# Layer 3 attention written out in order on three engines, with the router's logits on VectorE

## The chip, the cores and the metric

The kernel runs on one NeuronCore of one Trainium2 chip. The metric is device time in microseconds, the time of one launch; the median of several runs is given with the lowest and the highest. A profile is one further execution under the hardware profiler. Its span begins and ends with the program's instructions, so its own run time is a little longer than the span. The engines are called by the profile's names: PE is TensorE (PEld its weight loads), ACT ScalarE, DVE VectorE, POOL GpSimd, SP SyncE.

## The reference, cut to what matters

The network has four layers. The change concerns the last one, whose two parts work on 8 samples of 1024 tokens with 256 channels:

```python
def layer3_attention(x):                 # x: 8 x 1024 x 256
    q, k, v = heads(layernorm(x) @ qkv_w.T + qkv_b)        # 8 heads of 32 channels
    a = (q @ k.T * 32**-0.5 + 5.0) ** 2                    # a square in place of exp
    a = a / a.sum(-1, keepdims=True)
    return x + merge(a @ v) @ proj_w.T + proj_b

def layer3_experts(x):
    tokens = layernorm(x)
    probs = softmax(tokens @ router_w.T)                   # 8 experts
    rw, re = top_k(probs, 2)
    rw = rw / max(rw.sum(-1), 1e-12)
    out = tokens
    for e in range(8):
        h = gelu(tokens @ w1[e] + b1[e])
        out = out + combine[:, e] * (h @ w2[e] + b2[e])
    return x + out
```

This is a condensed form of the reference: bookkeeping (images to tokens, zero biases) is left out. Since a weight is a square of a sum, the sum of a row of `a` is a quadratic form in q, and needs no pass over the weights: with G = the sum over all keys of k times k transposed, head by head, the denominator of a query comes from q, Gq and the sum of the keys. The kernel uses this.

## The kernel before

Each layer is a Python generator that writes instructions; the `yield`s are places at which another generator may be let in. The framework then lays the instructions out, engine by engine, by a schedule of its own, except where a line pins them in program order (`net.pinned`). The order on an engine's queue is fixed when the program is built; at run time each engine works through its queue in order and waits on semaphores.

Layer 3's attention is `fast3` (from L2520), its router and the sorting of tokens by expert is the class `Routes`, and the experts are `fast3e`. Before attention starts, `fast3` loads its weights, normalises sample 0 beside the end of the layer before it (`norm`, L2567), waits for the point `HOLD` at which the other layer gives its space back (L2717), and then makes the products of sample 0 without attention beside it.

*Attention* (`attention`, L2655) does a sample in 32 steps: two halves of 512 queries, two groups of four heads (`c`), eight tiles of 128 keys (`kt`). A step has

- four score matmuls `s<-q,k` (L2686), one for each head, on rows 32h of the array, into two tiles of two PSUM banks each,
- two activations `e<-s` (L2692) on ScalarE, which square 128x1024 scores each,
- four value matmuls `A<-e,v` of the step before it (L2670), on columns 32h of the array, which add up in one bank over the eight key tiles. After the eighth, VectorE multiplies by the reciprocal denominator, `o<-A,r` (L2675). At the end of a half, PE projects four token tiles into a pair of banks, `proj<-o`, and VectorE adds them to x (`x<-proj,x`, L2681).

The scores and every other product take their tiles from one pool, `own["S"]`, of three tiles of two banks; `own["A"]` has two tiles of one bank. That is all eight banks.

*Beside attention* of sample b, `between(b)` (L2702) writes the router of sample b-1, the normalisation of sample b+1 and its products. `spread` (L1067) deals these pieces out over the 33 yields of `attention(b)`.

- `norm`: the load of x, statistics and normalisation on VectorE (`tn_s`, `tn_m`, `xt<-x,tn_r`), a logarithm and an exponential on ScalarE between them (`tn_r`), 16 transposes on PE (`xn<-ident,xt`) with two copies on VectorE, and the addition of the projection's bias to x on GpSimd (L2582, 128x2048).
- `projections`: q and k (each two pieces with an activation of 1024 columns), v (two pieces with a VectorE copy), the transposes of k (`kT`, two pieces with a VectorE copy), G, then Gq and the sums over a head D, two pieces each, with a VectorE product and two ScalarE functions behind them.
- `Routes.route` (L2380): a second normalisation (`mo_x`), stores of it and of x plus it (the addition on GpSimd, L2391), 16 transposes `mo_xT`, logits as 16 pairs of matmuls `mo_l`, the softmax and the choice of two experts by comparisons on VectorE, and two small matmuls `mo_n` that count the tokens ahead.
- `Routes.fill` (L2359), in sample 0 alone: six DMAs that fill the three tables of sorted rows with zeros, issued from SyncE.
- `Routes.sort` (L2462): in samples 3 and 6 the sorting of a group of three samples: loads of token tiles `xl<-mox` on SyncE and two indirect DMAs for each on GpSimd.

In the last sample the loads of the experts' weights (`net.head()`) stand in place of norm and products. After the loop, the router of the last sample goes beside the first experts: `by_time([[0, 1, some(all_pairs, lead)], [1, 1.1, routing]])` (L2951), where a stream is [first due time, time between pieces, generator].

An expert pair of blocks takes four or eight transposes (`a`), a VectorE copy `xk`, 8 matmuls `h`, a Gelu on ScalarE, matmuls `y`, two VectorE additions, and two indirect DMAs on GpSimd.

Of the kernel before, what the change touches and what calls it, by code (L numbers as in the profile page):

```python
# [17 lines left out]
P = 128  # L18
# [879 lines left out]
class Fast:  # L898
# [123 lines left out]

    def scatter(self, group, after=(), **args):


        made = self.nc.gpsimd.indirect_dma_start(**args)  # L1026
        self.pinned(made)
        ins = made.ins
        self.tc.declare_no_dep(ins, group=group, reason="rows of their own")
        self.tc.add_to_no_dep_group(group, ins)  # L1030
        self.wait_for(ins, after)
        self.groups.setdefault(group, []).append(ins)
# [9 lines left out]
    def pinned(self, *ins):  # L1042
        for i in ins:
            self.tc.keep_in_program_order(i)

# [1263 lines left out]
class Routes:  # L2309
# [28 lines left out]
    def load(self, wp):  # L2338

        net, nc = self.net, self.net.nc  # L2340
        self.wr = net.load(wp, "l3f_wr", "(k p) o -> p k o", p=P)
# [17 lines left out]
    def fill(self):  # L2359
# [8 lines left out]
        for g, so in enumerate(self.sorteds):  # L2368
            self.fills[g] = []
            for lo in range(0, TILES[g], 26):  # L2370
# [5 lines left out]
                self.net.pinned(ins)  # L2376
# [3 lines left out]
    def route(self, b, x, ones, pair):  # L2380
# [8 lines left out]
        yield from net.token_norm_steps(xn, x, two)  # L2389
# [3 lines left out]
        yield  # L2393
        xk = ones.tile([P, KC, N], F32, tag="xn", name="mo_xk")
        for c in range(KC):
            ps = pair("mo_xT").rearrange("p h n -> p (h n)")
            for t in range(NT):
                nc.tensor.transpose(ps[:, bass.ts(t, P)], xn[:, t, bass.ts(c, P)], net.ident)
            nc.vector.tensor_copy(xk[:, c, :], ps)
            yield  # L2400

        pr = two.tile([P, NT, E8], F32, tag="pr", name="pr")
        for t4 in range(0, NT, 4):
            ps = pair("mo_l")[:, 0]
            for i in range(4):
                net.linear(ps[:, bass.ts(i, E8)], xk, self.wr, bass.ts(t4 + i, P), slice(0, E8))
            nc.vector.tensor_copy(pr[:, t4 : t4 + 4], ps[:, : 4 * E8].rearrange("p (t e) -> p t e", e=E8))
            if not t4:
                yield
        red = two.tile([P, NT], F32, tag="red", name="red")  # L2410
        nc.vector.tensor_reduce(red, pr, AX.X, ALU.max)
        nc.vector.tensor_tensor(pr, pr, each(red), ALU.subtract)
        yield
# [11 lines left out]
        nc.vector.tensor_tensor(eq, other, mine, ALU.is_equal)  # L2425
        nc.vector.tensor_tensor(eq, eq, self.before.unsqueeze(1).to_broadcast([P, NT, E8, E8]), ALU.mult)
# [6 lines left out]
        for i in range(2):  # L2433
# [3 lines left out]
            nc.vector.tensor_reduce(weigh[:, i], tmp, AX.X, ALU.add)  # L2437
        nc.vector.tensor_tensor(red, weigh[:, 0], weigh[:, 1], ALU.add)
# [5 lines left out]
        yield  # L2444

        ps = pair("mo_n")[:, 0]
# [10 lines left out]
        for t in range(NT):  # L2457
            nc.vector.tensor_tensor(place[:, t], cnt[:, 0, t], carry, ALU.add)
            nc.vector.tensor_tensor(carry, carry, cnt[:, 1, t], ALU.add)
        yield  # L2460
# [59 lines left out]
def fast3(net, io):  # L2520
# [4 lines left out]
    with ExitStack() as ctx, ExitStack() as tok, ExitStack() as att, ExitStack() as bef:  # L2525
# [3 lines left out]
        def pair(name):  # L2529
            return net.lent["pair"](name) if not own else own["S"].tile([P, 2, HF], F32, tag="S", name=name)  # L2530

        def bank(name):
            return pair(name)[:, 0]
# [28 lines left out]
        xpool = io.pool(tok, "f3x", 3)  # L2562
        one = io.pool(tok, "f3a", 1)
        norms = io.pool(tok, "f3m", 2)
        xs, xns, qs, ks, vs, rs = ({} for _ in range(6))

        def norm(b):  # L2567
            x = xs[b] = xpool.tile([P, NT, C], F32, tag="x", name="x")

            (nc.sync if b else nc.scalar).dma_start(out=halves(x), in_=tokens(io.src[b]))  # L2570
            yield
            xt = one.tile([P, NT, C], F32, tag="xt", name="xt")
            yield from net.token_norm_steps(xt, x, norms, b > 0)
            yield
            xn = xns[b] = one.tile([P, KC, N], F32, tag="xn", name="xn")
            for c in range(KC):
                ps = pair("xn")
                for t in range(NT):
                    nc.tensor.transpose(ps[:, t // 4, bass.ts(t % 4, P)], xt[:, t, bass.ts(c, P)], net.ident)
                nc.vector.tensor_copy(xn[:, c, :], ps.rearrange("p h n -> p (h n)"))  # L2580
                yield
            nc.gpsimd.tensor_tensor(x, x, bo.unsqueeze(1).to_broadcast([P, NT, C]), ALU.add)  # L2582

        def projections(b):
            xn = xns.pop(b)
            for d, w, bias, name in ((qs, wq, bq, "q"), (ks, wkk, bk, "k")):
                d[b] = own["two"].tile([P, KC, N], F32, tag=name, name=name)
                for c in range(KC):
                    ps = pair("qk")
                    for h in range(2):  # L2590
                        net.linear(ps[:, h], w, xn, bass.ts(c, P), bass.ts(h, HF))
                    nc.scalar.activation(d[b][:, c, :], ps.rearrange("p h n -> p (h n)"), AF.Identity, bias=bias(c))
                    yield
            v = vs[b] = own["two"].tile([P, NT, C], F32, tag="v", name="v")
            for t4 in range(0, NT, 4):
                ps = pair("v")
                for i in range(4):
                    net.linear(ps[:, i // 2, bass.ts(i % 2, C)], xn, wv, bass.ts(t4 + i, P), slice(0, C))
                nc.vector.tensor_copy(
                    v[:, t4 : t4 + 4].rearrange("p t c -> p (t c)"), ps.rearrange("p h n -> p (h n)")  # L2600
                )
                yield


            kt = own["k1"].tile([P, NT, KC, P + 4], F32, tag="kt", name="kt")
            nc.gpsimd.memset(kt[:, :, :, P], 1.0)
            for t4 in range(0, NT, 4):
                ps = pair("kT")
                for i in range(4):
                    for c in range(KC):  # L2610
                        nc.tensor.transpose(
                            ps[:, i // 2, (i % 2) * C + c * P : (i % 2) * C + (c + 1) * P],
                            ks[b][:, c, bass.ts(t4 + i, P)], net.ident,
                        )
                nc.vector.tensor_copy(
                    kt[:, t4 : t4 + 4, :, :P], ps.rearrange("p h (i c n) -> p (h i) c n", c=KC, n=P)
                )
                yield
            G = bank("G").rearrange("p (c n) -> p c n", c=KC)
            for c in range(KC):  # L2620
                for t in range(NT):
                    nc.tensor.matmul(
                        G[:, c, : P + 1], lhsT=kt[:, t, c, :P], rhs=kt[:, t, c, : P + 1],
                        start=(t == 0), stop=(t == NT - 1),
                    )
            gm = own["k2"].tile([P, KC, P + 4], F32, tag="gm", name="gm")
            nc.vector.tensor_tensor(gm[:, :, : P + 1], G[:, :, : P + 1], heads.to_broadcast([P, KC, P + 1]), ALU.mult)
            yield
            prod = one.tile([P, KC, N], F32, tag="xt", name="prod")
            r = rs[b] = own["two"].tile([P, KC, N], F32, tag="r", name="r")  # L2630
            for c in range(KC):
                ps = pair("Gq")
                for h in range(2):
                    nc.tensor.matmul(
                        ps[:, h], lhsT=gm[:, c, :P], rhs=qs[b][:, c, bass.ts(h, HF)], start=True, stop=True
                    )
                nc.vector.scalar_tensor_tensor(
                    prod[:, c, :], ps.rearrange("p h n -> p (h n)"), gm[:, c, P : P + 1], qs[b][:, c, :],
                    ALU.add, ALU.mult,
                )  # L2640
                yield
            for c in range(KC):
                ps = pair("D")
                for h in range(2):
# [593 lines left out]
```

## Time and profile before

| | us |
|---|---|
| median of 3 runs | 4155.66 |
| lowest, highest | 4153.86, 4181.26 |
| the profiled execution, its span | 4178.96, 4177.1 |

Shares of the span, from the page:

| engine | busy us | share | instructions |
|---|---|---|---|
| PE | 3826.0 | 92% | 19430 |
| PEld | 1887.8 | 45% | 19430 |
| DVE | 2298.4 | 55% | 3994 |
| ACT | 2260.1 | 54% | 3030 |
| POOL | 566.3 | 14% | 646 |

The mean granted clock of TensorE was 0.954. Three stretches matter here (us from the start of the span; busy time in each):

| stretch | length | PE | DVE | ACT | POOL | clock |
|---|---|---|---|---|---|---|
| end of layer 2, start of layer 3 | 2700 to 2820 | 105.70 | 59.94 | 26.66 | 43.14 | 0.94 |
| attention of layer 3 | 2820 to 3800 | 961.70 | 290.00 | 608.42 | 173.62 | 0.99 |
| experts | 3800 to 4177 | 331.14 | 192.49 | 191.43 | 205.50 | 0.93 |

A busy time is the time in which at least one instruction of the engine was at work. Matmuls overlap, and a matmul that waits inside counts as busy, so 961.70 of 980 says that PE had something in hand nearly always, not that it went at full speed. In lists in order of time, a line gives the start, the length, the engine, the line of the kernel, the operation, what it writes and reads, shape and count, and in brackets how long the engine was idle before it and for whom it waited. One fp32 matmul leaves two records.

The groups that matter in the attention stretch (mean ns of one):

| group | count | mean ns |
|---|---|---|
| `e<-s`, ACT, 128x1024 | 512 | 1111 |
| `o<-A,r`, DVE, 128x512 | 32 | 689 |
| `x<-proj,x`, DVE, 128x1024 | 16 | 1225 |
| `kt<-kT`, `v<-v`, `xn<-xn`, `mo_xk<-mo_xT` copies, DVE, 128x1024 | 14 each | 1225 |
| `x<-x,mo_x` and `x<-x,bo`, POOL, 128x2048 | 8 each | 4537, 4522 |
| layer 2's router `junk<-xn,w_f_wr`, DVE, 128x256 with its accumulator read | 64 | 425 and 83 |
| ACT activation of a bank, 128x512 (`hp<-pi`) and copy (`u<-po`) | 128, 32 | 690, 585 |

### The profile page before, as it was taken

Reading aid. Unit: us, or ns where it says so; the run is one execution under the profiler, and the core shown is the slowest. Engines: PE = TensorE matmul, PEld = TensorE weight load, DVE = VectorE, ACT = ScalarE, POOL = GpSimd, SP = SyncE. Lnnn points to the kernel's source line nnn. Section 1 sums busy time; section 2 is a strip of 40 time slices with the busy share of each in tenths; the row PEclk is TensorE's granted clock in tenths of the full one; section 3 lists DMA queues with packets and bytes.
Section 4 is the critical chain, followed back from the end, with each engine's and each line's share of the span. In section 5 each row is a group of like instructions: output and inputs, shape, how many; then the busy total and the mean of one; then the engine's idle time right before and its main releaser. Section 6 shows DMA issues by size and latency. Waiting matters only on the chain. (4 is left out here: it accounts for less than half of the span.)

```text
span 4177.1 us, 51736 instructions
## 1 busy us (share of the span) xinstructions
PE 3826.0 (92%) x19430; PEld 1887.8 (45%) x19430; DVE 2298.4 (55%) x3994; ACT 2260.1 (54%) x3030; POOL 566.3 (14%) x646
## 2 busy tenths in 40 slices
PE   8999999999878787789999969989899999999987
PEld 3323333333334444454444526653344444346986
DVE  2398798798896489942222356841232333324445
ACT  4556555555553367734334346516566556666554
POOL 0000000000000000000000013430000050124753
PEclk9999999999998889889999979999999999999998
DMA  3313223223131568720000013430700040136676
GB/s 100 113 43 124 90 73 120 88 74 109 62 107 47 185 246 291 264 73 21 21 21 29 22 56 109 142 121 11 219 31 31 9 145 31 37 111 195 202 233 219
DMA packets 210069, 441.13 MB, mean 106 GB/s; under 512 B 22281, under 2 KB 132828, under 8 KB 197396
## 3 DMA queue, kind: packets, MB, share of 16 engines
q1 hardware_dynamic: 186708, 386.17, 28.1%
q0 software_dynamic: 19440, 46.45, 3.3%
q10 hardware_dynamic: 3664, 5.11, 0.4%
q8 instruction: 157, 2.57, 0.3%
q14 instruction: 100, 0.82, 0.1%
HBM read 282.30 MB, written 162.28 MB: 106 GB/s over the span
## 5 line engine op out<-in xcount | busy, mean ns | idle before, releaser
L2692 ACT ACTIVATE e<-s,five 128x1024 f32<-128x1024 f32 x512 | 539.3, 1111 | 280.0 <-PE s L2686 279.2
L1249 DVE SCALAR_TENSOR_TENSOR a<-hp,w_f_vec,a 128x961 f32<-128x961 f32 (+1 forms) x496 | 608.7, 1233 | 115.3 <-ACT a L1242 106.7
L2686 PE MATMUL s<-q,k 32*128 32x512 f32 x2048 | 349.1, 644 | 16.3 <-ACT e L2692 12.1
L1401 ACT ACTIVATE e<-s 128x1024 f32<-128x1024 f32 x256 | 250.2, 1023 | 79.4 <-PE s L1395 62.8
L2670 PE MATMUL A<-e,v 128*32 128x512 f32 x2048 | 279.0, 609 | 0.0
L1355 DVE TENSOR_TENSOR sum<-sum,e 128x1024 f32<-128x1024 f32 x192 | 230.6, 1220 | 87.2 <-ACT e L1401 87.2
L78 PE MATMUL pi<-xn,w_l_wpi 128*128 128x512 f32 x512 | 249.0, 629 | 19.2 <-ACT v L1283 10.0
L1359 PE MATMUL A<-e,va 128*32 128x512 f32 x2048 | 263.0, 610 | 0.0
L2686 PEld LDWEIGHTS s<-q,k 32*128 32x128 f32 x2048 | 111.4, 184 | 179.4 <-issue 96.2
L1395 PE MATMUL s<-q,k 32*128 32x512 f32 x1024 | 181.2, 650 | 2.5 <-ACT e L1401 2.5
L78 PEld LDWEIGHTS pi<-xn,w_l_wpi 128*128 128x128 f32 x512 | 96.7, 199 | 161.9 <-issue 118.2
L2839 PE MATMUL h<-xk,w 128*128 128x128 f32 x1192 | 150.7, 281 | 19.0 <-DVE xk L2825 19.0
L1706 PE MATMUL acc<-wt,z 128*64 128x192 f32 (+4 forms) x1344 | 128.9, 334 | 42.4 <-DVE wt L1761 42.0
L1026 POOL DMA_INDIRECT res<-y,to x149 | 148.4, 996 | 106.6 <-DVE y L2863 47.7
L2839 PEld LDWEIGHTS h<-xk,w 128*128 128x128 f32 x1192 | 148.3, 197 | 24.1 <-DVE xk L2825 19.3
L2808 ACT COPY w<-w_l3f_w 128x512 f32 x149 | 92.6, 625 | 119.6 <-PE h L2839 116.3
L1440 ACT ACTIVATE hp<-pi,pib 128x512 f32<-128x512 f32 x128 | 87.2, 690 | 127.3 <-PE pi L78 127.2
L1310 POOL MEMSET thrice<- 32x128 f32 x32 | 6.3, 196 | 1021.7 <-PE pe L1326 1021.6
L2859 PE MATMUL y<-w_l3f_w,hid 128*128 x596 | 142.8, 382 | 0.3 <-ACT hid L2845 0.3
L1026 POOL DMA_INDIRECT so<-xl,rows x128 | 129.9, 1015 | 93.0 <-issue 51.0
L1706 PEld LDWEIGHTS acc<-wt,z 128*64 128x64 f32 x1344 | 97.7, 151 | 89.5 <-DVE wt L1761 60.1
L1359 PEld LDWEIGHTS A<-e,va 128*32 128x32 f32 x2048 | 57.6, 111 | 174.2 <-issue 172.9
(407 smaller groups left out, 6966.5 us busy)
## 6 DMA issues: line engine op xcount, KB each, us to landing
row<-shifts SPq DMA_DIRECT2D x144, 512.0 KB
x<-d SPq DMA_DIRECT2D x31, 1024.0 KB
xs<-so SPq DMA_DIRECT2D x73, 260.0 KB
so<-zero SPq DMA_DIRECT2D x5, 3380.0 KB
thrice<-vimg SPq DMA_DIRECT2D x64, 256.0 KB
gated<-st SPq DMA_DIRECT2D x32, 512.0 KB
hc<-gated SPq DMA_DIRECT2D x32, 512.0 KB
xl<-mox SPq DMA_DIRECT2D x64, 256.0 KB
```

What stands on the lines that cost most here:

```text
L78: self.nc.tensor.matmul(ps, lhsT=w[:, i, m], rhs=src[:, i, cols], start=(i == 0), stop=(i == k - 1))
L1026: made = self.nc.gpsimd.indirect_dma_start(**args)
L1249: nc.vector.scalar_tensor_tensor(to, fr, taps(t_), to, ALU.mult, ALU.add)
L1355: nc.vector.tensor_tensor(half, half, e[j], ALU.add)
L1359: nc.tensor.matmul(state["A"][32 * h : 32 * h + 32, c, :], lhsT=vas[b][:, kt, c, 32 * h : 32 * h + 32], rhs=e[h // 2][:, h % 2, :], start= ...
L1395: nc.tensor.matmul(ss[h // 2][:, h % 2], lhsT=ks[b][32 * h : 32 * h + 32, bass.ts(kt, P)], rhs=qs[b][32 * h : 32 * h + 32, bass.ts(gq, HF) ...
L1401: nc.scalar.activation(es[i][j], ss[j], AF.Exp, scale=SCALE)
L1706: nc.tensor.matmul(acc[o, a * IMG : e * IMG], lhsT=zs[b][:, c, t, :], rhs=wt[:, c, (a - lo) * IMG : (e - lo) * IMG], start=False, stop=(t ...
L2670: nc.tensor.matmul(A[32 * h : 32 * h + 32], lhsT=v[:, kt, c * P + 32 * h : c * P + 32 * h + 32], rhs=e[:, h, :], start=first, stop=last,)
L2686: nc.tensor.matmul(ss[h // 2][:, h % 2], lhsT=k[32 * h : 32 * h + 32, c, bass.ts(kt, P)], rhs=q[32 * h : 32 * h + 32, c, bass.ts(hh, HF)], ...
L2692: nc.scalar.activation(e[:, 2 * j : 2 * j + 2], ss[j], AF.Square, scale=SCALE, bias=five)
L2839: nc.tensor.matmul(ps[:, j, m], lhsT=ws[j][:, k, bass.ts(m, P)], rhs=xk[:, j, k], start=(k == 0), stop=(k == KC - 1),)
```

## The change

- The attention loop is one loop over 256 steps of all samples (`attention(beside, parts)`), under `net.in_order(PE, DVE, Activation)`: each instruction of these three engines is made to follow the one written before it on its engine.
- Products come in pieces of one bank. `denominators` is split from `projections`; k comes before q. The pieces take their bank from a new pool `own["X"]` of one bank; `own["A"]` shrinks from two tiles to one. A step writes one piece after the values (or a quarter of a sample's projection, one and two steps after the step that follows a half's end), and a further one before the values where the number of the piece is in `SMALL`.
- The copies of the transposes of x (`turned`) and of k go from VectorE to ScalarE.
- The heads of a step are written in the order 2, 3, 0, 1, for scores and values.
- The load of x (`fetch`) is a piece of its own, two samples ahead, at step 10; the normalisation, in small pieces (`token_norm_pieces`), from step 15. Samples 0 and 1 are normalised before the loop.
- The router's logits are 64 multiply-and-sum instructions on VectorE, from a table `f3_wr` of the router's weights repeated on all partitions (1 MB), in place of transposes and matmuls.
- The six fills are written at steps 10, 19, 28, ... and each waits for the last square written before it.
- After the loop, the pieces of the last router come due every 0.26 instead of 1.1.

The core of the diff:

```diff
+    @contextmanager
+    def in_order(self, *engines):
+        traced = self.nc.cur_bb.bb.instructions
+        start = len(traced)
+        yield
+        info = mybir.DependencyInfo(mybir.DependencyClass.NoSync, mybir.DependencyReason.DATA)
+        for engine in engines:
+            last = None
+            for i in traced[start:]:
+                if i.engine == engine:
+                    if last is not None:
+                        self.tc.add_manual_dep(i, last.name, info, reason="as planned")
+                    last = i
...
-                self.net.pinned(ins)
+                self.net.wait_for(ins.ins, [a.ins for a in anchor])
...
-        xk = ones.tile([P, KC, N], F32, tag="xn", name="mo_xk")
-        for c in range(KC):
-            ps = pair("mo_xT").rearrange("p h n -> p (h n)")
-            for t in range(NT):
-                nc.tensor.transpose(ps[:, bass.ts(t, P)], xn[:, t, bass.ts(c, P)], net.ident)
-            nc.vector.tensor_copy(xk[:, c, :], ps)
-            yield
...
+        junk = one.tile([P, C], F32, tag="junk", name="junk")
+        for t in range(NT):
+            for e in range(E8):
+                nc.vector.scalar_tensor_tensor(
+                    junk, xn[:, t, :], 1.0, self.wr[:, e, :], ALU.mult, ALU.mult, accum_out=pr[:, t, e : e + 1]
+                )
+                if e % 2:
+                    yield
...
+        def turned(b, h, c):
...
+            ps = bank("xn")
+            for t in range(4):
+                nc.tensor.transpose(ps[:, bass.ts(t, P)], xts[b][:, 4 * h + t, bass.ts(c, P)], net.ident)
+            nc.scalar.copy(xns[b][:, c, bass.ts(h, HF)], ps)
...
-            for i, (hh, c, kt) in enumerate(steps):
-                ss = [pair("s") for _ in range(2)]
-                for h in range(NH):
+            for i, (b, hh, c, kt) in enumerate(steps):
+                ss = [own["S"].tile([P, 2, HF], F32, tag="S", name="s") for _ in range(2)]
+                for h in LATEST:
...
+                run(i, beside)
+                turn = bool(projects) and projects[0][0] <= i
+                if not turn and parts and parts[0][0] <= i and parts[0][1] in SMALL:
+                    piece()
                 if i:
                     values(i - 1)
-                yield
+                if projects and projects[0][0] <= i:
+                    project(*projects.pop(0)[1:])
+                elif parts and parts[0][0] <= i:
+                    piece()
...
+        LATEST = (2, 3, 0, 1)
+        SMALL = (12, 14, 26)
...
-        own["S"], own["A"] = io.pool(att, "f3s", 3, PSUM), io.pool(att, "f3v", 2, PSUM)
+        own["S"], own["A"] = io.pool(att, "f3s", 3, PSUM), io.pool(att, "f3v", 1, PSUM)
...
+        for i, _ in enumerate(denominators(0)):
+            if 3 <= i < 7:
+                turned(1, (i - 3) // 2, (i - 3) % 2)
+        own["X"] = io.pool(att, "f3o", 1, PSUM)
...
+            if b + 1 < B:
+                parts.append([at + (3 if b else 0), 0, products(b + 1)])
+            if b + 2 < B:
+                beside.append([at + 9, 1, later(1, (fetch(n) for n in (b + 2,)))])
+                beside.append([at + 15, 1, norm(b + 2)])
+            if b:
+                beside.append([at + 3, 0.48, routed(b - 1)])
+            if b == 0:
+                beside.append([at + 10, 9, routes.fill(anchor)])
...
+        with net.in_order(mybir.EngineType.PE, mybir.EngineType.DVE, mybir.EngineType.Activation):
+            attention(beside, parts)
...
-        by_time([[0, 1, some(all_pairs, lead)], [1, 1.1, routing]])
+        by_time([[0, 1, some(all_pairs, lead)], [1, 0.26, routing]])
```

`run(i, beside)` lets in every stream of `beside` that is due at step i; `piece()` writes the next one-bank piece of the products; `products(b)` are `projections(b)`, `denominators(b)` and the four transposes of sample b+1, 30 pieces in all.

## The prediction

> **What bounds the kernel now.** I read first the page's slices, to find the stretch that the change touches, then the table of stretches, then the instructions in order of time. Attention of layer 3 runs from its first score matmul (2819.65 us) to the last addition of the projection (3798.79): 979.1 us of the profiled span of 4177.1. In that stretch the table reads:
>
> ```profile
> 2960.00:3000.00 40.00, 28.82 (x194) 9.47 (x197) 15.20 (x64) 23.17 (x25) 0.00 (x0) 0.86 0.85 270
> 3160.00:3200.00 40.00, 40.00 (x242) 18.50 (x240) 8.59 (x8) 21.78 (x21) 0.32 (x2) 1.00 0.00 1
> 3720.00:3760.00 40.00, 40.00 (x272) 17.32 (x272) 6.54 (x14) 26.50 (x26) 29.39 (x36) 0.96 0.58 184
> ```
>
> Columns: stretch, length, busy time of TensorE, its weight loads, VectorE, ScalarE, GpSimd, then the granted clock, DMA share, GB/s. TensorE (PE) is full but for one stretch, VectorE under half. A full PE may still wait inside its matmuls, so I went to the order of time. Three places tell what a step costs. A step with a piece beside it:
>
> ```profile
> 3154.75 1.14 PE L2686 MATMUL s<-q,k 32*128 32x512 f32 x8
> 3155.82 1.07 PE L2670 MATMUL A<-e,v 128*32 128x512 f32 x8
> 3156.82 3.70 PE L78 MATMUL qk<-xn,w_l_wk 128*128 128x512 f32 x8
> 3160.45 1.14 PE L2686 MATMUL s<-q,k 32*128 32x512 f32 x8
> ```
>
> By the starts, scores take 1.07 us, values 1.00 and this piece 3.63; nothing waits. (Records come two to a matmul.) So an attention step costs PE 2.07, while ScalarE squares it in 2.12 (two activations). The end of a half sample is different:
>
> ```profile
> 3200.13 1.44 PE L2670 MATMUL A<-e,v 128*32 128x512 f32 x8
> 3201.50 0.70 PE L78 MATMUL proj<-w_l_wo,o 128*128 128x256 f32 x2
> 3202.13 1.12 PE L2686 MATMUL s<-q,k 32*128 32x512 f32 x2
> 3203.18 3.29 PE L78 MATMUL proj<-w_l_wo,o 128*128 128x256 f32 x14
> 3206.40 1.13 PE L2686 MATMUL s<-q,k 32*128 32x512 f32 x6
> 3207.79 2.06 PE L2686 MATMUL s<-q,k 32*128 32x512 f32 x8 [0.25 <-DVE x L2681]
> 3209.78 1.06 PE L2670 MATMUL A<-e,v 128*32 128x512 f32 x8
> ```
>
> From 3200.13 to the end of the last line's work (3210.78) are 10.65 us for two steps (4.13) and a projection (3.86): 2.65 lost, because the projection takes a pair of banks that scores need. And once PE stands still:
>
> ```profile
> 2949.15 21.98 SPq L2372 DMA_DIRECT2D so<-zero  x3
> 2988.10 0.33 SPq L2570 DMA_DIRECT2D x<-d  x1
> 2995.14 0.43 DVE L1003 BATCH_NORM_STATS2 tn_s<-x 128x6 f32<-128x256 f32 x1 [15.46 <-DMA x<-d]
> 2997.29 2.08 PE L2686 MATMUL s<-q,k 32*128 32x512 f32 x4 [11.18 <-ACT e L2692]
> ```
>
> The zero fills hold the SyncE queue, the load of the next sample comes late behind them, VectorE's statistics wait for it, ScalarE's logarithm for those, the squares behind the logarithm, and PE for the squares.
>
> **The sum of before.** Pieces of one sample, by the same reading of starts: transposes of x 2x1.02, q and k 4x3.63, v 2x3.66, transposes of k 2x1.02, G 3.76, Gq 2x1.92, D 2x1.92, together 37.4; projection 2x3.86 = 7.7; router 6.4 (transposes 2x1.02, logits 2x1.88, counts 0.6). With 256 steps at 2.065: 528.6 + 7x37.4 + 8x7.7 + 7x6.4 = 897 us of PE. The other 82: projection ends 16x2.65 = 42, the hole 11.7, some 100 steps without a piece at about 2.27 instead of 2.07 = 20, start and rest 8. It closes.
>
> **The change, part by part.**
> *Router off PE.* Its transposes and logits leave: 5.8 us x7 in the loop = -40.6. In place of them stand 64 multiply-and-sum instructions per sample on VectorE. The nearest row is layer 2's router, same shape: 0.43 us plus an accumulator read, 0.54 from start to start: 34.6 us per sample, about 4.2 of them (2.25 us) per step. VectorE then has some 67 us per sample of about 117; per step 2.25 + statistics 0.8 + a copy 0.69 = 3.7 at the densest, against PE steps of 3.9 with a q, k or v piece and 3.0 with Gq. So it is covered, with up to 0.7 us over in three Gq steps, which the next steps absorb. If the cover goes, each us over is a us of PE, since the only accumulator bank waits for VectorE.
> *A rule against it.* No row here has an operation with two SBUF inputs on VectorE beside a GpSimd addition. The Trainium skill, SBUF — State Buffer, "Who interferes with whom", states that these two exclude each other for a whole instruction. GpSimd's x + normed x (4.54 us) starts just when the router's sums start. By the row alone 0; by the rule VectorE stands 4.5 us late once per sample, of which PE sees about 1 (the bank is needed some 3 us later and the rest is regained): +8. I take +4.
> *One-bank pieces, one per step.* PE's work is the same; the two-bank transfers are halved (512 columns: 0.69 against 1.23 for 1024), more instructions on engines with room. Projection in two pieces, two steps after the half's end, in a bank of its own: -42. Nearly every step has a piece: 28 free steps and three double ones (kT, kT, transposes) hold 30 pieces. Steps without a piece: of 100, about 35 remain (most in the last sample): -13.
> *What is new there.* All pieces share one bank. In a double step the second piece waits for the copy of the first, which stands behind both squares on ScalarE: scores 1.07, latency 0.2, squares 2.12, copy 0.6 = 4.0 us after the step's start, PE is ready at 2.6: 1.5 lost, 2.4 where exponentials of D stand before it. Per sample 1.5+1.5+2.4 = 5.4, less 0.5 that ScalarE-bound transposes lose today; 5x4.9, 4.9 for sample 0, 3.0 for sample 6: +32. In single steps the bank is free in time: the copy ends 4.0 to 4.6 after the step's start, the next piece starts 5 to 6 after it.
> *Heads 2, 3 first.* They need the buffer that the step's first square frees, so with no piece beside it a step is a chain: square 1.04, scores 1.07, four latencies of 0.1: about 2.45 instead of 2.27. Some 35 such steps: +6.
> *Copies of x and k on ScalarE.* Eight copies of 0.6 per sample. ScalarE then works 32x2.12 + 20x0.6 + exponentials 2 = 83 of 117 us. Nothing but the double steps.
> *Fills behind anchors, loads two samples ahead.* The fills come nine steps apart (35 us, each holds SyncE 7) and the load of sample b+2 is due five steps before its statistics: the hole goes, -11.7. What is late next: this load stands on SyncE behind the store of x + normed x of sample b-1 and, for sample 3, behind a fill and two sort loads; I count 0 to +5, take 2.
> *Before the loop.* Norm, transposes and load of sample 1 move ahead. In VectorE's order eight additions of layer 2 (4.70 us, their gathers done by 2758) now stand between the first six and last two normalisations of sample 0: the second half of xn comes at 2788 instead of 2784. The 16 extra transposes (2.0) leave the loop's first sample. +4 (0 to 8).
> *After the loop.* The last router runs beside the first experts: seven sums (3.8) per pair of blocks, with xk 0.69 and y 0.95 are 5.4 on VectorE against 3.95 for PE, for nine pairs: +13, less 4 that three xk buffers cover, less what the PE router costs there today (seven pairs took 34.0 instead of 27.7, from h at 3802.5 to 3836.5: 6.4, part of which, table loads, stays: 3). +6 (0 to 13).
> GpSimd's scatters of the sorts stand in another order past two of its additions; they end with the loop either way. A 1 MB router table is loaded in place of a small one, in layer 2's stage, hidden by its work.
>
> Sum in the loop: -40.6 -42 -13 +32 +6 +4 -11.7 +2 = -63, to about 916; replaying one middle sample step by step gives 117.5 us and the whole loop 910. I take -66. With +4 and +6: -56. The profiled execution was 4178.96 (1.96 beside its span), the median of the runs 4155.66, 0.56% less; the difference is carried over to the median: 4155.66 - 56 = **4100 us**.
>
> **The rivals.**
> *The new bank and VectorE take half of it back* (0.23). Were twelve short pieces with ScalarE copies per sample (D, kT, transposes) held 0.5 us each, it would be 12x0.5x7 = +42: 4142. For it: one bank, two queues in front of it. Against: the margins of 1 us above.
> *All of the stalls vanish* (part of the forecast's upper side, 0.2): double steps cost PE nothing and the post-loop router is hidden: -56 -32 -6 = 4062.
> *A late load stops VectorE in written order* (0.05, the slower side). VectorE's statistics of sample b+2 stand ahead of the release of the accumulator. By its place in the order the load can leave when x + normed x is stored, some ten steps (38 us) into a sample, and the statistics stand at step 15 (58 us): with the 6 us that a load takes, 14 us of slack; each us beyond it stops PE, as the 11.18 did. To end over 1% slower it must cost 56 + 42 = 98 us, 16 in each of six samples, so come 30 us late. Against: today the store leaves at 3344.82, as soon as GpSimd's addition (3340.26, 4.53 long) ends, and a load lands within some 6 us of its issue.
> *The order is already what is written.* PE's order of before is nearly regular, so only router and hole might count: -40.6 -11.7 +10 = -42: 4113. It lies inside the range.
>
> **How the numbers follow.** About 1% (42 us) is what a measurement can tell. Forecast and its upper side 0.72 (4060 to 4120), half back 0.23, late load 0.05. The range 4060 to 4138 leaves out about 0.2. Faster by over 1% means below 4114: 0.70; within 1%: 0.26; slower 0.04.
>
> **What would show it.** The hole between 2985 and 2997 gone; scores at 1.07 in every step with a piece; no projection beside which scores wait; double kT steps of 4.6 us with PE waiting for the copy; samples of 117 to 118 us instead of 125; the last sample 86 instead of 90; h matmuls 5.4 us apart for the first nine pairs. Wrong would be: long VectorE waits for x, or PE waiting for the bank in single steps.

## The result, and the profile after

The changed kernel took 4107.87 us (median of 4 runs, 4106.14 to 4110.10); the kernel before took 4163.95 beside it (4 runs). The ratio is 0.9861, with a 95% interval of 0.9823 to 0.9900, so 1.4% faster. The forecast was 4100, range 4060 to 4138.

The profiled executions differ by more, 4177.1 against 4108.3 us of span, and 16.8 of these 68.8 lie ahead of layer 3: the matmul of the projection's bias (`bo`) starts at 2769.7 before and at 2753.0 after. Of what lies ahead of it the change touches only the load of a larger table, and in the runs below `bo` starts anywhere from 2750 to 2800. I count from there. "Loop" is the time from the start of the first score matmul to the start of the last record of the last projection:

| stretch | before | after | difference | forecast |
|---|---|---|---|---|
| `bo` to the first scores | 49.9 | 51.9 | +2.0 | +4 |
| loop | 978.7 | 921.5 | -57.3 | -66 |
| behind the loop | 378.8 | 382.0 | +3.2 | +6 |

Only the loop's difference is large against what else moves: in the runs below, the stretch behind the loop takes 378 to 399 us with one and the same code, by the chip, so +3.2 is not shown to be a cost. The loop itself hardly depends on the chip: sample 2 takes 124.5 us in the kernel before and in `h_fills`, which ran on another one and has the same code there.

Table of stretches, after (columns as before: stretch, length, busy time of TensorE, weight loads, VectorE, ScalarE, GpSimd, clock, DMA share, GB/s):

```profile
2960.00:3000.00 40.00, 37.62 (x237) 16.69 (x238) 24.47 (x99) 24.45 (x26) 0.00 (x0) 1.00 0.42 127
3160.00:3200.00 40.00, 40.00 (x218) 13.22 (x215) 19.56 (x57) 28.00 (x32) 4.64 (x1) 1.00 0.19 72
```

The stretch with the hole has 37.62 us of TensorE instead of 28.82 and a full clock instead of 0.86. VectorE works 24.47 us there instead of 15.20; in the other stretch, where no hole was, 19.56 instead of 8.59, more than twice as much.

Instructions of the changed kernel in order of time: a step with a piece, a doubled step (two pieces), a step with a projection:

```profile
3185.29 1.14 PE L2745 MATMUL s<-q,k 32*128 32x512 f32 x8
3186.36 1.06 PE L2725 MATMUL A<-e,v 128*32 128x512 f32 x8
3187.35 1.98 PE L78 MATMUL qk<-xn,w_l_wq 128*128 128x512 f32 x4
3189.27 1.14 PE L2745 MATMUL s<-q,k 32*128 32x512 f32 x8
...
3217.17 1.14 PE L2745 MATMUL s<-q,k 32*128 32x512 f32 x8
3218.24 0.66 PE L2659 MATMUL kT<-ident,k 128*128 128x128 f32 x4
3218.83 1.07 PE L2725 MATMUL A<-e,v 128*32 128x512 f32 x8
3221.09 0.66 PE L2659 MATMUL kT<-ident,k 128*128 128x128 f32 x4 [1.19 <-ACT kt L2662]
3221.68 1.14 PE L2745 MATMUL s<-q,k 32*128 32x512 f32 x8
...
3227.25 1.06 PE L2725 MATMUL A<-e,v 128*32 128x512 f32 x8
3228.24 1.99 PE L78 MATMUL proj<-w_l_wo,o 128*128 128x256 f32 x8
3230.17 1.14 PE L2745 MATMUL s<-q,k 32*128 32x512 f32 x8
```

By the starts, a quarter of q takes 1.92 us (3187.35 to 3189.27), where half of a two-bank piece was 1.815. The doubled step lasts 4.51 and its second piece waits 1.19 for ScalarE's copy. The projection is a piece like any other, 1.93, and no score waits. A middle sample lasts 118.6 us instead of 124.5 to 126.5; the last one, from its first score to the last record of the loop, 95.5 instead of 93.9.

What VectorE does beside GpSimd's long addition, in samples 1 and 7:

```profile
2950.80 4.63 POOL L2428 TENSOR_TENSOR x<-x,mo_x 128x2048 f32<-128x2048 f32 x1 [36.01 <-DVE mo_x L1041]
2951.10 4.62 DVE L2435 SCALAR_TENSOR_TENSOR junk<-mo_x,w_f_wr 128x256 f32<-128x256 f32 x1
2953.03 1.06 PE L2725 MATMUL A<-e,v 128*32 128x512 f32 x8
2955.65 0.68 DVE L2730 TENSOR_TENSOR o<-A,r 128x512 f32<-128x512 f32 x1
2957.01 1.07 PE L2725 MATMUL A<-e,v 128*32 128x512 f32 x8
...
3657.27 5.26 DVE L2435 SCALAR_TENSOR_TENSOR junk<-mo_x,w_f_wr 128x256 f32<-128x256 f32 x1
3657.71 4.53 POOL L2428 TENSOR_TENSOR x<-x,mo_x 128x2048 f32<-128x2048 f32 x1
3678.71 0.69 DVE L2730 TENSOR_TENSOR o<-A,r 128x512 f32<-128x512 f32 x1
3679.54 1.94 PE L2725 MATMUL A<-e,v 128*32 128x512 f32 x8 [3.38 <-DVE o L2730]
```

One router sum, 0.42 us elsewhere, ends 0.29 us after the addition, in both places. In sample 1 TensorE's values keep their distance of 3.98 all the same. In sample 7, where steps have no piece and last 2.40, VectorE works off its sums until 3678.7 and TensorE waits 3.38 for the accumulator.

### The profile page after: what moved, and what is told of

It is laid out like the page before. It is cut to its first block, busy times and chain, and to the rows that moved or that the text cites. A ratio compares the mean times of both kernels' runs of the same rounds, so it can differ in the third digit from the quotient of the medians.

```text
span 4108.3 us, 52125 instructions
## 1 busy us (share of the span) xinstructions
PE 3745.4 (91%) x19046; PEld 1810.0 (44%) x19046; DVE 2510.4 (61%) x5010; ACT 2306.0 (56%) x3142; POOL 569.1 (14%) x646
## 5 line engine op out<-in xcount | busy, mean ns | idle before, releaser
L2745 PE MATMUL s<-q,k 32*128 32x512 f32 x2048 | 306.1, 641 | 0.0
L2435 DVE SCALAR_TENSOR_TENSOR junk<-mo_x,w_f_wr 128x256 f32<-128x256 f32 x512 | 250.2, 489 | 13.3
L78 PE MATMUL pi<-xn,w_l_wpi 128*128 128x512 f32 x512 | 240.6, 611 | 14.7 <-ACT u L1539 9.2
L1432 PE MATMUL s<-q,k 32*128 32x512 f32 x1024 | 179.9, 649 | 2.5 <-ACT e L1438 2.5
L2745 PEld LDWEIGHTS s<-q,k 32*128 32x128 f32 x2048 | 91.0, 183 | 147.1 <-issue 142.2
```

The source lines that it names most:

```text
L78: self.nc.tensor.matmul(ps, lhsT=w[:, i, m], rhs=src[:, i, cols], start=(i == 0), stop=(i == k - 1))
L2435: nc.vector.scalar_tensor_tensor(junk, xn[:, t, :], 1.0, self.wr[:, e, :], ALU.mult, ALU.mult, accum_out=pr[:, t, e : e + 1])
L2745: nc.tensor.matmul(ss[h // 2][:, h % 2], lhsT=ks[b][32 * h : 32 * h + 32, c, bass.ts(kt, P)], rhs=qs[b][32 * h : 32 * h + 32, c, bass.ts(h ...
```

## The experiments

All are compared with the kernel before on the same chip; it took 4155 to 4230 us from chip to chip, so times are given as ratios, and the loops from the traces, one of each run. "Idle" is the part of the loop in which TensorE has nothing in hand (a matmul that waits inside counts as busy), "half clock" the time in the loop in which its granted clock was 0.5; otherwise it was 1.0. All in us.

| run | from | loop | idle | half clock | ratio to the kernel before, interval |
|---|---|---|---|---|---|
| the kernel before | | 978.7 | 17.1 | 23.9 | 1 |
| the change | | 921.5 | 29.7 | 6.8 | 0.9861 (0.9823 to 0.9900) |
| a_router_only | before | 1043.9 | 98.0 | 129.7 | 1.0162 (1.0145 to 1.0179) |
| p_proj_bank | before | 990.2 | 30.4 | 27.3 | 1.0001 (0.9992 to 1.0011) |
| h_fills | before | 964.9 | 5.2 | 10.2 | 0.9951 (0.9934 to 0.9967) |
| b_no_order | after | 1054.7 | 110.7 | 129.7 | 1.0184 (1.0152 to 1.0216) |
| r1_dve_order | after | 923.2 | 9.2 | 6.8 | 0.9860 (0.9833 to 0.9887) |
| r2_router_order | before | 1065.8 | 70.0 | 139.9 | 1.0188 (1.0166 to 1.0209) |
| i_late_exp | before | 1057.2 | 108.3 | 119.5 | 1.0220 (1.0186 to 1.0254) |
| c_two_doubles | after | 910.2 | 22.4 | 3.4 | 0.9838 (0.9816 to 0.9861) |
| d_gq_doubles | after | 910.0 | 18.0 | 13.7 | 0.9839 (0.9807 to 0.9870) |
| best1 | after | 935.4 | 32.6 | 23.9 | 0.9910 (0.9887 to 0.9934) |
| e_split | after | 938.1 | 29.9 | 6.8 | 0.9898 (0.9872 to 0.9925) |
| f_heads_0123 | after | 915.3 | 29.6 | 3.4 | 0.9856 (0.9828 to 0.9885) |

The last but one column shows a cost that the forecast did not have. Behind the hole of the kernel before, the clock is 0.5 from 2988.8 to 3002.5, and the values last 1.94 us instead of the usual 1.07:

```profile
2999.29 1.94 PE L2670 MATMUL A<-e,v 128*32 128x512 f32 x8
```

The step with the hole lasts 17.34 us, the same step of the next sample 3.07: 11.18 of the difference are the wait, 3.1 the clock behind it. Below, I estimate the clock's cost as half of the time in which TensorE works at half clock. Every stretch of 10 us or more at half clock in these loops begins within a wait of TensorE. What sets the clock was not tested: a short wait has half clock behind it in some places and not in others.

**Three parts of the change, each alone on the kernel before.** The router:

```diff
-        xk = ones.tile([P, KC, N], F32, tag="xn", name="mo_xk")
...
+        for t in range(NT):
+            for e in range(E8):
+                nc.vector.scalar_tensor_tensor(
+                    junk, xn[:, t, :], 1.0, self.wr[:, e, :], ALU.mult, ALU.mult, accum_out=pr[:, t, e : e + 1]
+                )
+            yield
```

> The kernel before with one part of the change: logits as 64 multiply-and-sum instructions on VectorE. The sum's term: 5.8 us of TensorE per sample go, -40.6 in the loop, some +6 behind it, so 35 us faster than before. Rival: the 64 sums now stand in one block of 34.6 us on VectorE, two accumulator banks cover only eight steps (about 30 us), so TensorE waits 5 to 10 us per sample for o<-A: gain of 0 to 10 us, or none.

It is 1.6% slower, the loop 65 us longer. Neither the term nor the rival has the mechanism. Waits of this kernel (engine, for whom, us in total, times, longest):

```profile
PE s L2679 <- ACT e L2685: 87.6, 14, 14.6
ACT pr L2406 <- DVE pr L2404: 86.1, 6, 15.5
```

and in order of time, sample 2:

```profile
3113.84 2.12 ACT L2685 ACTIVATE e<-s,five 128x1024 f32<-128x1024 f32 x2 [0.16 <-PE s L2679]
3130.21 0.26 ACT L2406 ACTIVATE pr<-pr 128x64 f32<-128x64 f32 x1 [14.26 <-DVE pr L2404]
3131.52 2.08 PE L2679 MATMUL s<-q,k 32*128 32x512 f32 x4 [13.34 <-ACT e L2685]
```

ScalarE's small exponential of the router (`pr`, 0.26 us) stands in ScalarE's order ahead of the next squares, and waits for 64 sums that the schedule put in one block on VectorE. TensorE waits behind the squares: it is the hole of before (a logarithm waiting for statistics), six times over. The bank wait that I had named as the rival came to no more than 7.0 us. The term itself is there, but buried: 80.9 us more of idle TensorE and, as an estimate, 23 more for the half clock (17.1 us at each of the six waits), less 40.6, make +63.5.

The projection in a bank of its own, one accumulator bank instead of two:

```diff
-                        ps = pair("proj")
...
+                        projects.extend((i + 2 + t2 // 2, hh, t2) for t2 in (0, 2))
...
+                if projects and projects[0][0] <= i:
+                    project(*projects.pop(0)[1:])
...
-        own["S"], own["A"] = io.pool(att, "f3s", 3, PSUM), io.pool(att, "f3v", 2, PSUM)
+        own["S"], own["A"] = io.pool(att, "f3s", 3, PSUM), io.pool(att, "f3v", 1, PSUM)
```

> The kernel before with one part of the change: the projection of a half in two pieces in a bank of its own (one accumulator bank instead of two), written two and three steps after the half for the first half of a sample, at the sample's end for the second. The sum's term: 2.65 us for each of 16 projection ends, 42 us faster. Rival: the pair of banks was not the cause, the wait for o<-A and for the addition was; then a delay of two steps helps the first halves alone, and one accumulator bank costs 1 us each eight steps: gain of 0 to 15 us.

No gain at all; the loop is 11 us longer. The rival's low end held, and its two parts can be told apart. At the ends of first halves, which have the delay, scores no longer wait; at the ends of samples, which have not, two steps and the projection still take 10.8 us (10.65 before). And the second accumulator bank is missed:

```profile
PE A L2670 <- DVE o L2675: 19.7, 8, 3.0
```

In six samples this wait is 2.9 to 3.0 us long; `o<-A` stands behind the router's comparisons in VectorE's order. The first halves had less to give than the sum says: in sample 2 the three steps at their end take 12.16 us instead of 13.75, so 1.6 are gained; the 2.65 were read at the end of a sample. With the wait that sample is 1.4 us longer than before. Of the 11 us, some 8 are sample 4, where 10.2 us passed at half clock.

The fills:

```diff
-                self.net.pinned(ins)
+                self.net.wait_for(ins.ins, [a.ins for a in anchor])
...
+            if b == 0:
+                beside.append((later(1, routes.fill(anchor)), 7))
```

> The kernel before with one part of the change: the six zero fills spread over sample 0, each behind the last square written before it, instead of in a row. The sum's term: TensorE's stand of 11.18 us near 2997 goes, 11.7 us faster and nothing else moves. Rival: the load is late for another reason or the next thing in the queue is as late: no change, the stand stays.

As the sum had it, and a little more: the loop is 13.8 us shorter, the wait and the half clock behind it. The wait, one of 11.18 us before, is now

```profile
PE s L2686 <- ACT e L2692: 1.2, 2, 1.0
```

**The order.**

```diff
-        with net.in_order(mybir.EngineType.PE, mybir.EngineType.DVE, mybir.EngineType.Activation):
-            attention(beside, parts)
+        attention(beside, parts)
```

> The changed kernel without the fixed order on the three engines; the rest of the change stays. The rival 'the order already is what is written': the framework's schedule differs on TensorE only in the doubled steps, so the time stays within 5 us of the changed kernel's (4108, loop 923 us). If the fixed order carries the gain at the projection ends: 40 us slower than the changed kernel.

The loop is 133 us longer, more than twice the gain. TensorE's order differs in the doubled steps only, as expected; the conclusion from it was wrong. Waits:

```profile
PE A L2725 <- DVE o L2730: 72.1, 9, 10.1
PE v L78 <- DVE v L2648: 34.3, 6, 10.1
```

TensorE waits for VectorE's releases of the accumulator and of the pieces' bank, which stand behind some 26 sums in a row. So I fixed VectorE alone:

```diff
-        with net.in_order(mybir.EngineType.PE, mybir.EngineType.DVE, mybir.EngineType.Activation):
+        with net.in_order(mybir.EngineType.DVE):
```

> The changed kernel with the fixed order on VectorE alone; TensorE's order is then that of the kernel without any fixed order, VectorE's in the loop that of the changed kernel. If what the kernel without fixed order lost (133 us of loop) was VectorE's order, with 64 router sums in one block ahead of the releases of the accumulator and of the pieces' bank: loop 923 us and the time within 5 us of the changed kernel's, some 61 faster than before. If TensorE's or ScalarE's order carried it: as slow as without, 70 us slower than before.

All but one of these waits (4.6 us) are gone, VectorE's order in the loop is that of the change throughout, and the ratio, 0.9860, is that of the change as well. Of the 133 us that the fixing brings, VectorE's order is all but some 2. About 32 of them are the clock, by the estimate above.

**Can the router go to VectorE in the kernel before, if the order is right?** First VectorE in written order, four sums to a piece:

```diff
+                if e % 4 == 3:
+                    yield
...
+        with net.in_order(mybir.EngineType.DVE):
```

> The kernel before with the router's sums on VectorE, four sums to a piece, and VectorE alone kept in written order in the attention stage. If the block of sums was what made the router slower there by 65 us of loop, the sum's term comes out: 30 to 41 us of loop less than before. If the sums on VectorE cost TensorE in themselves (a shared port, a bank that is never free in time), it stays slower than before by 20 us or more; a written order that is bad elsewhere (products crowded into the last 14 steps) would show as waits for ScalarE's squares.

A miss: 1.9% slower. The block was not broken up by it: in six samples VectorE still does 32 sums in a row (in most of them twice), because almost nothing else stands between the pieces in its written order. ScalarE still waits for the router's values (42.1 us in six waits, 7.9 the longest), TensorE another 16.9 for the counts. TensorE is idle 52.9 us longer than before and loses some 50 more to the half clock; less 40.6, that is 63 of the 87 us, and the other 24 stay open. Then the exponential moved away from the sums:

```diff
-                yield from routes.route(b - 1, xs[b - 1], one, pair)
+                yield from routes.logits(b - 1, xs[b - 1], one)
...
+                beside.append((later(16, routes.choose(b - 1, pair)), 24))
```

> The kernel before with the router's sums on VectorE in one block, as in the first such run, but with the router's exponential and choice written in the last third of the sample, so that ScalarE's exponential no longer stands in front of squares while the sums run. If what made the router slower there was that ScalarE waited with 86 us in six samples for the sums' end: these waits go, loop 1044 less 80 = 960, that is about 20 us less than before. If the accumulator's release behind the block is as bad: it takes the exponential's place as the wait, loop above 1010. The whole term of the sum (-40.6) would be a loop of 938.

A miss as well, for a reason that is of use. The waits at `pr` are gone, but the next small ScalarE function that needs VectorE has taken their place, the logarithm of the norm, whose statistics now stand behind the block of sums (the last one starts at 3109.26):

```profile
3110.75 0.30 ACT L1008 ACTIVATE tn_r<-tn_m,eps 128x8 f32<-128x8 f32 x1 [11.61 <-DVE tn_m L1006]
```

TensorE's scores then wait 10.98 us for the squares at 3112.34, and there are five such waits of ScalarE, 58.0 us together. In sample 4 TensorE also waits 24.33 us for the normalised x, which VectorE writes. Moving one of them does not help while the sums are a block.

**Terms of the sum, in the changed kernel.** Two doubled steps instead of three:

```diff
-        SMALL = (12, 14, 26)
+        SMALL = (12, 14)
```

> The changed kernel with two doubled steps per sample instead of three (the transposes of x are no longer doubled). By the working of the prediction: the doubled step of 5.07 us and the step without a piece of 2.4 become two steps of 2.7 and the count's 0.6: 1.4 us less in six samples, 8 to 9 us faster than the changed kernel, 4099. Rival: the last copy of x turned now comes one step before k needs it and k waits: no gain, or up to 2 us per sample slower.

The loop is 11.3 us shorter, more than expected; 3.4 of it are sample 0, where the change waits 1.72 us at its doubled transposes and then passes 3.4 us at half clock, and this kernel does neither. A middle sample gains 1.6. The transposes of x, one to a step:

```profile
3263.29 0.66 PE L2629 MATMUL xn<-ident,xt 128*128 128x128 f32 x4
3263.88 1.14 PE L2745 MATMUL s<-q,k 32*128 32x512 f32 x8
3264.95 1.06 PE L2725 MATMUL A<-e,v 128*32 128x512 f32 x8
3265.94 0.66 PE L2629 MATMUL xn<-ident,xt 128*128 128x128 f32 x4
```

Steps of 2.65, no wait. In the loop this version beats both kernels; as a ratio, its gain over the change (0.9838 against 0.9861) lies inside the intervals.

Doubled steps at Gq instead:

```diff
-        SMALL = (12, 14, 26)
+        SMALL = (18, 20)
...
-                beside.append([at + 15, 1, norm(b + 2)])
+                beside.append([at + 18, 1, norm(b + 2)])
```

> The changed kernel with the doubled steps at Gq (whose bank VectorE frees) instead of at the transposes of k and x (whose bank ScalarE frees behind two squares); the normalisation of sample b+2 starts three steps later, since the transposes of k end later. If the doubled steps' loss is the wait for ScalarE: a doubled Gq step takes 4.1 us, kT steps 2.7 each, 2.4 us per sample less and the 1.4 of the third doubled step: 24 us faster than the changed kernel, 4084. Rival: VectorE's router sums stand in front of Gq's product, so the bank waits as long for VectorE: no change, 4105 to 4110.

Half of it came: 11.4. The kT steps are 2.65 as expected, but the first doubled Gq waits for VectorE (below), and in samples 2 and 3 the router's count, reached sooner, waits 2.13 and 2.21 for `both`, with 6.8 and 3.4 us at half clock behind it. These two samples take 121.3 and 120.0 us where samples 1, 4 and 5 take 116.1 to 116.2: 9 of the 12.6 us that are missing.

```profile
3240.05 1.12 PE L2680 MATMUL Gq<-q,gm 128*128 128x512 f32 x2
3241.11 1.07 PE L2725 MATMUL A<-e,v 128*32 128x512 f32 x8
3243.72 1.13 PE L2680 MATMUL Gq<-q,gm 128*128 128x512 f32 x2 [1.54 <-DVE prod L2681]
```

So I put the doubled steps where I thought VectorE free, and one copy of x on VectorE:

```diff
-        SMALL = (12, 14, 26)
+        SMALL = (20, 27)
...
+            copy = nc.vector.tensor_copy if own and (h, c) == (0, 1) else nc.scalar.copy
```

> The changed kernel with two doubled steps per sample, at pieces 20 (the third Gq, freed by VectorE) and 27 (transposes of x, whose copy goes to VectorE when the router there is over), the normalisation two steps later and the count of the router two and a half steps later. If the doubled kT steps' waits for ScalarE and the wait for the count are what is left: no bank wait at all in doubled steps, 1.2 us less for each of two kT steps and the 1.4 of the third doubled step: loop 892 to 898, 25 to 30 us faster than the changed kernel, about 4080. If VectorE has no room at these places: loop 905 to 912, as with two doubled steps alone.

Worse than the change by 14 us of loop: in place of the 16.7 us that the change waits for the copies of kT, TensorE waits 15.4 for Gq's products, and 5.9 for the accumulator. So VectorE, though busy only 498 of the 935 us, has no room in these steps. The idle time alone is just 2.9 us longer than the change's; the half clock, behind four of the waits for Gq, one for the accumulator and one for the squares, costs some 8.5 more by the estimate.

Each q, k and v piece in two parts, with the values between them:

```diff
-                        net.linear(ps, w, xn, bass.ts(c, P), bass.ts(h, HF))
+                        for i in range(KC):
+                            if i:
+                                yield
...
-        SMALL = (12, 14, 26)
+        SMALL = tuple(range(0, 24, 2)) + (24, 26, 38)
```

> The changed kernel with each q, k and v piece cut in two parts of equal work, one before and one behind the values of its step; same matmuls, same bank, 84 more passages between matmuls of a part of the array (scores, values) and of the whole array. If each passage costs TensorE about 0.1 us for going in and 0.1 for coming out: steps of 4.07 to 4.17 us instead of 3.98, 8 to 16 us slower than the changed kernel. If passages are free and the 0.1 us per piece seen in the trace is something else: 3.98 and no change.

The loop is 16.6 us longer, and a step is 4.18 instead of 3.98:

```profile
3183.39 1.14 PE L2753 MATMUL s<-q,k 32*128 32x512 f32 x8
3184.46 1.12 PE L2643 MATMUL qk<-xn,w_l_wk 128*128 128x512 f32 x2
3185.52 1.07 PE L2733 MATMUL A<-e,v 128*32 128x512 f32 x8
3186.51 1.12 PE L2643 MATMUL qk<-xn,w_l_wk 128*128 128x512 f32 x2
3187.57 1.14 PE L2753 MATMUL s<-q,k 32*128 32x512 f32 x8
```

16.6 over 84 parts is 0.20 us for each further visit of the whole array; how it divides into going in and coming out was not separated. Scores use the array by rows and values by columns, so a part between them adds two passages and takes away the direct one; 0.20 is what is left of the three. Each part takes 1.06, 0.10 more than half of 1.92.

The heads in order 0, 1, 2, 3:

```diff
-        LATEST = (2, 3, 0, 1)
+        LATEST = (0, 1, 2, 3)
```

> The changed kernel with the heads of a step in the order 0, 1, 2, 3. The sum's term had the order 2, 3, 0, 1 cost 6 us (steps without a piece of 2.45 instead of 2.27): loop 915 instead of 921. Rival: with 0, 1 first the two heads run ahead alone and 2, 3 wait for the buffer that the first square frees, so the four no longer run side by side where ScalarE is late (scores of 1.46 instead of 1.14, as in steps without a piece of the kernel before): loop the same or up to 10 us longer.

The loop is 6.2 us shorter, as the sum's term had it; but 1.7 of it are the 3.4 us at half clock in sample 0, which this kernel has not. Some 4.5 are the order. Steps without a piece, this kernel:

```profile
3671.95 1.14 PE L2745 MATMUL s<-q,k 32*128 32x512 f32 x8
3673.02 1.07 PE L2725 MATMUL A<-e,v 128*32 128x512 f32 x8
3674.02 1.51 PE L2745 MATMUL s<-q,k 32*128 32x512 f32 x8
3675.46 1.07 PE L2725 MATMUL A<-e,v 128*32 128x512 f32 x8
3676.46 1.14 PE L2745 MATMUL s<-q,k 32*128 32x512 f32 x8
```

and the changed kernel:

```profile
3648.35 1.48 PE L2745 MATMUL s<-q,k 32*128 32x512 f32 x8
3649.75 1.06 PE L2725 MATMUL A<-e,v 128*32 128x512 f32 x8
3650.75 1.48 PE L2745 MATMUL s<-q,k 32*128 32x512 f32 x8
```

2.26 a step (4.51 for two) against 2.40. Two scores do run ahead here, but only in each second step, so the rival is refuted. With two doubled steps this was not tried together.

## Why the prediction was right, point by point

The total was right, and the places were: hole, projection ends, kT steps of 4.5, no late loads. That it agrees so closely (56.1 us between the medians for a forecast of 56) is luck: the loop gained 9 us less than forecast and the stretches outside it cost 5 less, and the profiled executions differ by 12.7 us more than the medians.

*VectorE's order.* This is what the prediction left out. It costed the router on VectorE as covered because VectorE is half idle, and its fourth rival judged what an order is worth by TensorE's alone. Covered it is only in the written order: in the schedule's order the same instructions make the loop 133 us longer. So -40.6 for the router and -42 for the projection are no gains of these edits alone, which measured +65 and +11. For the router the gain shows only with a VectorE order in which no release and no small input of ScalarE stands behind a block of sums. How much each edit brings inside the changed kernel stays a sum: no run has that kernel with the router left on TensorE, or without its new projection.

*Projection, -42.* Too much by its own reading: 2.65 is the end of a sample, the end of a first half lost about 1.6, so 16 ends make 34.

*The clock.* The sum has waits, but no cost of the half clock behind them. In the changed kernel that is about 3 us, in the runs with long waits 24 to 58.

*Fewer steps without a piece, -13, and "PE's work is the same".* Mis-sized. A two-bank q step and an empty one took 5.70 + 2.27 = 7.97 before; two one-bank steps take 2 x 3.98 = 7.96. By the starts, each one-bank piece is 0.08 to 0.10 longer than half of a two-bank piece (projections excepted): 2.7 us a sample, 19 in seven, which the sum did not have. The run with split pieces shows that it goes with the number of parts: a visit costs 0.20, and each half carries a whole one. The Trainium skill, TensorEngine Tiling (Array Packing), "Key Properties", states that a change of the tiling mode drains TensorE. It gives no price; whether the drain or any break between groups of matmuls costs the 0.20 was not separated. It is the rule against this change that I had not weighed.

*Doubled steps, +32.* Right in kind (4.51 for 4.6; 1.19 of waiting for ScalarE), somewhat too high: TensorE waits 16.7 us there for kT and 7.2 for the transposes of x. Taking the third one away gave 11.3.

*Heads 2, 3 first, +6.* 6.2 measured, about 4.5 of it the order.

*Hole, -11.7.* 13.8 measured, with the half clock.

*The lock of VectorE and GpSimd, +4.* The rule of the Trainium skill, SBUF — State Buffer, "Who interferes with whom", is seen: the sum lasts 4.62 us beside an addition of 4.63, where the row alone would have had 0.42. Only in sample 7 the sum's record starts 0.44 us before the addition's and is held all the same, though the page lets the order of issue decide who waits; why stays open. And the profile of before did have a row for it: of the eight additions `s<-yg,m,s` that the prediction gives as 4.70 us, both inputs in SBUF, the first lasts 1.93 us where the median is 0.48, until GpSimd's addition (2782.49, 4.51 long) has ended. The lock's price for TensorE was nothing in sample 1, where VectorE's slack took it up. In the last sample VectorE comes 3.38 late; that the 4.6 us are the reason is argued, not tried.

*The last sample.* Forecast 4 us shorter (86 for 90), measured 1.6 longer: the wait of 3.38, 3.4 us at half clock behind it, and 2.40 for most of its steps. *Middle samples.* 118.6 for 117.5, where the passages are. These two make 5.6 + 6 x 1.1 = 12 us, about the distance between the replayed loop (910) and 921.5.

*Behind the loop.* +3.2 for +6, less than chips differ by, and not in the form forecast: h matmuls of the first 15 pairs stand 4.42 us apart (3730.34 to 3792.23), not 5.4 for nine; the sums are spread thinner than I had read.

## What to carry to other kernels

Work moved to a half idle engine is hidden only if, in that engine's own order, nothing that others wait for stands behind it: read there what releases a bank and what feeds a small function on a third engine, before counting busy time. When an edit depends on such an order, test it without the order too; its gain may be the order's. Many small pieces between matmuls of another tiling are not free, even with no wait in the trace. And a wait can cost more than its length: look at the granted clock behind it.

## What the runs showed of the hardware

- One more visit of the whole array between scores and values cost TensorE 0.20 us (84 added parts, 16.6 us), with no wait shown in the trace.
- At a granted clock of 0.5 the values took 1.94 us instead of 1.07. Loops with long waits passed 119.5 to 139.9 us at half clock, the changed kernel's 6.8.
- A VectorE multiply-and-sum of two SBUF operands (0.42 us) that meets a GpSimd addition (4.5 to 4.6 us) ended about 0.3 us after it: 4.62 long in the changed kernel, 4.63, 4.64 and 4.65 in three of the other runs, and 5.26 in sample 7.
- The multiply-and-sum with its accumulator read takes 0.47 us from start to start, not the 0.54 that I took from layer 2.
